# Attention with the scores made twice: once by query for their maxima, once by key for the exponentials

## The chip, the core and the metric

The kernel runs on one core of one Trainium2 chip. The metric is device time in microseconds (us) of one execution of the whole program; lower is better. PE is the matrix engine (PEld its weight loads), DVE the vector engine, ACT the scalar engine with the activation functions, POOL the general-purpose engine, SP the engine whose queue issues all DMA transfers of this kernel.

## What is computed

Two layers run over `x` of shape (4, 512, 512), each with a cross mixer and a feed-forward part, each part added to the residual through a tanh gate. Layer 0 is a recurrent "wkv" scan and a feed-forward part with ternary-sign weights and activations quantised in groups of 64. Layer 1 is cross-attention with 16 heads of 32 channels and a ternary linear layer. The change touches the attention alone:

```python
q = _qdq(x) @ _qdq(wq).T + bq            # x: layer-normed residual, (4, 512, 512)
kv = cond @ wkv.T + bkv
k, v = jnp.split(kv, 2, axis=-1)          # 16 heads of 32 channels each
scale = 1.0 / np.sqrt(Dh)
attn = jax.nn.softmax(jnp.einsum('bnhd,bmhd->bhnm', q, k) * scale, axis=-1)
o = jnp.einsum('bhnm,bmhd->bnhd', attn, v).reshape(B, N, C)
out = _qdq(o) @ _qdq(wp).T + bp           # _qdq: round to int8 steps and back
```

## The kernel before

The four batches pass through the stages one behind the other. While batch b is in attention, batch b+1 is in its feed-forward part and batch b+2 in its scan; the main program walks along a line of places (`line`, `place`, `run`) and lets each generator make its next step when its place comes. The last batch's attention (`alone`) has no feed-forward part beside it. Within PE the order of these steps is fixed: the helpers `matmul` (L162) and `transpose` (L165) put every PE instruction behind those of the step before (`in_turn`, `next_turn`), so a PE instruction that waits holds up all that follow. The other engines also take their instructions in order, and SP issues DMAs in order.

Attention of a batch is 16 units of work: 8 pairs of heads (p), each for two halves of the 512 queries (h); a unit is 2 heads (i) by 2 tiles of 128 queries (t). Queries and keys are kept in DRAM as two parts each, a rounded one and its remainder, so that a product of the fast type float32r keeps accuracy. `stack` (L892) loads them as stacked row blocks of 32: keys as (0, 1, 0, 1), queries as (0, 0, 1, 1), four DMAs each, so that one product over 128 rows sums all four cross terms.

A unit takes these steps, over three turns of the unit loop (L1041 to L1079):

- `scores` (L916): for each i and t one product of 128 queries by 512 keys into a PSUM bank of the group "hp" (3 banks, shared with the feed-forward part's `ff_hp`); DVE takes each row's negated maximum (`at_nm`, L927); ACT takes exp with that as bias, sums the row on the way and writes the weights with queries on partitions (`at_P`, L929).
- `turned` (L937), one turn later: PE transposes the weights, four 128x128 blocks for each i and t, into a bank of group "m" (3 banks; "acc" when alone), and ACT copies them to SBUF (`at_PT`, L949); when alone, DVE makes half of the copies (L947).
- `values` (L952), two turns later: 16 products with 32 columns of V each, four of them side by side in the array (each is two PE instructions in the profile), then an ACT copy (`at_os`).
- `collect` (L971): one transpose back, a reciprocal of the row sums and a product by it (DVE, into `at_o`).

`fetch_queries` asks for the queries of unit k+2, `fetch_keys` for the keys of the next pair of heads. The feed-forward part loads its weights (`wT`, 1 MB each, L704) through the same SP queue; its products are `ff_hp` and `ff_acc`, its transposes `tp_ps`. `qr_ps`, `sx_ps`, `q_ps`, `p_ps`, `f_ps` belong to the projections before and after attention.

Of the kernel before, what the change touches and what calls it, by code (L numbers as in the profile page):

```python
# [10 lines left out]
F32 = mybir.dt.float32  # L11
F32R = mybir.dt.float32r
# [4 lines left out]
ALU = mybir.AluOpType  # L17
# [4 lines left out]
P = 128  # L22
# [8 lines left out]
def kernel(  # L31
# [42 lines left out]
    QSCALE = 1.0 / math.sqrt(DH)  # L74
    GS = 64
    ROWS = 3
    NG = D // GS

    cp = ctx.enter_context(tc.tile_pool(name="const", bufs=1))
# [81 lines left out]
    def matmul(*args, **kwargs):  # L161
        return in_turn(nc.tensor.matmul(*args, **kwargs))  # L162

    def transpose(*args):
        return in_turn(nc.tensor.transpose(*args))  # L165

    def blocks(a):
        return a.rearrange("p (c q) -> p c q", q=P)
# [651 lines left out]
    def attention_layer(b, xb, pool, tiles=range(NT)):  # L820
# [40 lines left out]
        qR, kR, V, PT, sums, made, lanes, out_s = {}, {}, {}, {}, {}, {}, {}, {}  # L861

        def rows(a):
            return slice(DH * a, DH * (a + 1))
# [24 lines left out]
        def stack(dst, src, order):  # L889

            for a, i in enumerate(order):
                nc.sync.dma_start(  # L892
                    out=dst[rows(a), :, :].bitcast(F32),
                    in_=src[i].rearrange("(j p) t -> p j t", p=DH),
                )

        def pair(p):
            return slice(64 * (p % 2), 64 * (p % 2) + 64)

        def fetch_keys(p):  # L900
            kR[p] = pool.tile([P, 2, T], F32R, name="at_kR", tag="at_kR")
            stack(kR[p], kD[b][p // 2][:, pair(p), :], (0, 1, 0, 1))

        def fetch_queries(k):
            p, h = units[k]
            qR[k] = pool.tile([P, 2, 2 * P], F32R, name="at_qR", tag="at_qR", bufs=3)
            at = lo + 2 * P * h
            stack(qR[k], qD[b][p // 2][:, pair(p), at : at + 2 * P], (0, 0, 1, 1))

        def fetch_values(g):  # L910
            V[g] = pool.tile([P, NT, P], F32, name="at_V", tag="at_V")
# [4 lines left out]
        def scores(k, i, t):  # L916

            p, h = units[k]
            if k not in sums:
                sums[k] = sm.tile([P, 2, 2], F32, name="at_sum", tag="at_sum")  # L920
            at = t * P
            sp = psum_tile("s_ps", "hp")
            matmul(
                sp, lhsT=qR[k][:, i, at : at + P], rhs=kR[p][:, i, :], start=True, stop=True
            )
            nm = sm.tile([P, 1], F32, name="at_nm", tag="at_nm", bufs=8)
            nc.vector.tensor_reduce(nm, sp, AX.X, ALU.max, negate=True)  # L927
            lanes[k, i, t] = pool.tile([P, T], F32, name="at_P", tag="at_P", bufs=6)
            nc.scalar.activation(  # L929
                lanes[k, i, t],  # L930
                sp,
                AF.Exp,
                bias=nm,
                accum_out=sums[k][:, t, i : i + 1],
            )

        def turned(k, i, t):  # L937

            if k not in PT:
                PT[k] = pool.tile([P, 2, NT, 2 * P], F32, name="at_PT", tag="at_PT", bufs=1)  # L940
            w = lanes.pop((k, i, t))
            pt = psum_tile("pt_ps", "acc" if alone else "m")
            for m in range(NT):
                transpose(pt[:, m * P : (m + 1) * P], w[:, m * P : (m + 1) * P], ident)
            dst = PT[k][:, i, :, t * P : (t + 1) * P]
            if alone and i:
                made[k] = nc.vector.tensor_copy(dst, blocks(pt))  # L947
            else:
                made[k] = nc.scalar.copy(dst, blocks(pt))  # L949

        def values(k):


            p, h = units[k]
            acc = bank("o_ps")[:, 0:P]
            for m in range(NT):
                for i in range(2):
                    for t in range(2):
                        mm = matmul(
                            acc[rows(2 * i + t), :],  # L960
                            lhsT=V[p // 2][:, m, rows(2 * (p % 2) + i)],
                            rhs=PT[k][:, i, m, t * P : (t + 1) * P],
                            start=(m == 0),
                            stop=(m == NT - 1),
                        )
                        behind(mm, made[k])
            del PT[k]
            out_s[k] = pool.tile([P, P], F32, name="at_os", tag="at_os", bufs=1)
            nc.scalar.copy(out_s[k], acc)  # L969

        def collect(k):  # L971

            p, h = units[k]
            pt = bank("ot_ps")[:, 0:P]
            transpose(pt, out_s.pop(k), ident)
            rt = sm.tile([P, 2, 2], F32, name="at_rt", tag="at_rt")
            nc.vector.reciprocal(rt, sums.pop(k))
            at = tiles[0] + 2 * h
            nc.vector.tensor_tensor(
                o_all[:, at : at + 2, p * 64 : p * 64 + 64].rearrange(  # L980
                    "p t (i d) -> p t i d", d=DH
                ),
                pt.rearrange("p (i t d) -> p t i d", i=2, d=DH),
                rt.unsqueeze(3).to_broadcast([P, 2, 2, DH]),
                ALU.mult,
            )
# [51 lines left out]

        for k in range(len(units) + 2):  # L1041
            now, before = k < len(units), 0 < k <= len(units)
            for i in range(2):
                if now:
                    scores(k, i, 0)
            yield
            if k > 1:
                values(k - 2)
            next_turn()
            for i in range(2):  # L1050
                if before:
                    turned(k - 1, i, 0)
            if alone and k > len(units):
                next_turn()
                next(ahead)
            yield
            for i in range(2):
                if now:
                    scores(k, i, 1)
            yield  # L1060
            for i in range(2):
                if before:
                    turned(k - 1, i, 1)
            next_turn()
            if k > 1:
                collect(k - 2)
            if now:
                p, h = units[k]
                if h == 0:
                    if p + 1 < NP:  # L1070
                        fetch_keys(p + 1)
                    if p % 2 == 0 and p // 2 + 2 < NC:
                        next_turn()
                        project(p // 2 + 2)
                elif p % 2 and p // 2 + 1 < NC:
                    fetch_values(p // 2 + 1)
                if k + 2 < len(units):
                    fetch_queries(k + 2)
            yield  # L1079

        if alone:
# [313 lines left out]
```

## Time and profile before

| | |
|---|---|
| median of 3 runs | 1110.24 us (1108.35 to 1112.83) |
| the profiled execution | 1115.4 us, span 1113.6 us |
| PE busy | 946.8 us (85%) |
| DVE busy | 851.9 us (76%) |
| ACT busy | 704.8 us (63%) |
| POOL busy | 315.3 us (28%) |
| mean granted PE clock | 0.953 |

The span is one execution as the hardware profiler saw it. The busy shares are averages over stages of different make. The first product of attention starts at 380 us; the attention of the four batches begins at about 380, 588, 810 and 983 us, and from 983 us on there is no other batch beside it. In a row of the trace's timeline, the first number is the start (us from the span's start), the second the time from the first instruction's start to the last one's end; matmuls overlap their neighbours, so the price of a burst on PE is read from its start to the start of what follows. Behind "|" or in brackets stands idle time before an instruction and what ended it.

### The profile page before, as it was taken

What the parts mean: (1) busy time and instruction counts of PE and PEld (TensorE: products, weight loads), DVE (VectorE), ACT (ScalarE), POOL (GpSimd) and SP (SyncE); (2) the same over time, 40 slices, a digit from 0 to 9 for tenths busy, and PEclk for the clock granted to TensorE, in tenths of its full rate; (3) what the DMA queues carried; (4) which work ended last, traced back from release to release, by engine and by line L of the source; (5) the groups of instructions that cost most, each with busy time, mean ns of one, the idle gap of its engine ahead of it and who ended that gap; (6) DMA issues with size and microseconds to landing.
All of it is one profiled execution on the core that took longest, in us unless ns stands there. A gap on an engine that the chain in (4) does not pass through costs nothing.

```text
span 1113.6 us, 17974 instructions
## 1 busy us (share of the span) xinstructions
PE 946.8 (85%) x6380; PEld 683.5 (61%) x6380; DVE 851.9 (76%) x1642; ACT 704.8 (63%) x1454; POOL 315.3 (28%) x311
## 2 busy tenths in 40 slices
PE   4879998978878978889998777899998989878885
PEld 3345565555546756667776466677776767656652
DVE  4986447779776799988759988877687766679977
ACT  6756655453224676667777667577775677877864
POOL 3822104432105143542214536412113321100000
PEclk8879999998888999999999999999998999989997
DMA  8189854554435655644746544466564653253411
GB/s 283 50 275 319 305 199 147 179 170 152 151 104 170 226 188 161 195 152 158 246 153 209 178 152 152 145 213 199 170 197 152 225 193 109 71 158 106 114 49 39
DMA packets 85673, 189.68 MB, mean 170 GB/s; under 512 B 12240, under 2 KB 36816, under 8 KB 74576
## 3 DMA queue, kind: packets, MB, share of 16 engines
q1 hardware_dynamic: 85584, 188.53, 51.5%
q8 instruction: 51, 0.84, 0.3%
q14 instruction: 38, 0.31, 0.1%
HBM read 148.65 MB, written 39.85 MB: 169 GB/s over the span
## 4 chain that ended last, share of the span: by engine, by line
PE 44%; DVE 25%; ACT 12%; issue 8%; POOL 6%; DMA 3%; SPq 1%; POOLq 0%; ACTq 0%; DVEq 0%
PE ff_hp L162 13%; PE ff_acc L162 6%; PE pt_ps L165 5%; PE o_ps L162 4%; PE s_ps L162 3%; PE v_ps L162 3%; DVE wk_q L620 3%; ACT at_P L929 3%; DVE at_nm L927 3%; ACT at_PT L949 2%; PE k_ps L162 2%; PE tp_ps L165 2%; DVE wk_p L614 2%; DVE qg_i L660 1%; PE qr_ps L165 1%
## 5 line engine op out<-in xcount | busy, mean ns | idle before, releaser
L162 PE MATMUL ff_hp<-wT,xp 128*128 128x512 f32 x1024 | 273.7, 411 | 3.7 <-ACT at_P L929 2.1
L162 PEld LDWEIGHTS ff_hp<-wT,xp 128*128 128x128 f32 x1024 | 197.4, 196 | 52.4 <-ACT at_P L929 3.8
L929 ACT ACTIVATE at_P<-s_ps,at_nm 128x512 f32<-128x512 f32 x256 | 174.6, 689 | 74.6 <-DVE at_nm L927 70.9
L927 DVE TENSOR_REDUCE at_nm<-s_ps 128x1 f32<-128x512 f32 x256 | 165.6, 676 | 37.8 <-PE s_ps L162 37.2
L665 POOL TENSOR_TENSOR ff_z<-qg_b,qg_s 128x512 f32<-128x512 bf16 x64 | 71.4, 1116 | 333.0 <-ACT qg_b L664 286.6
L165 PE MATMUL pt_ps<-ident,at_P 128*128 128x128 f32 x1024 | 141.1, 278 | 17.5 <-ACT at_os L969 6.6
L949 ACT COPY at_PT<-pt_ps 128x512 f32<-128x512 f32 x224 | 124.5, 595 | 39.7 <-PE pt_ps L165 38.5
L165 PEld LDWEIGHTS pt_ps<-ident,at_P 128*128 128x128 f32 x1024 | 113.2, 140 | 45.6 <-issue 9.3
L162 PE MATMUL ff_acc<-wT,hr 128*128 128x512 f32 x512 | 136.9, 408 | 4.9 <-ACT hr L676 3.0
L162 PE MATMUL s_ps<-at_kR,at_qR 128*128 128x512 f32 x256 | 98.8, 455 | 22.2 <-ACT at_P L929 14.6
L162 PEld LDWEIGHTS ff_acc<-wT,hr 128*128 128x128 f32 x512 | 92.6, 190 | 25.5 <-ACT hr L676 4.1
L725 ACT ACTIVATE ff_z<-ff_hp,coef 128x512 f32<-128x512 f32 x64 | 43.9, 687 | 65.8 <-PE ff_hp L162 63.2
L162 PE MATMUL o_ps<-at_PT,at_V 128*32 128x128 f32 x2048 | 72.2, 279 | 1.3 <-DVE hr L677 0.7
L664 ACT CAST qg_b<-qg_i 128x512 bf16<-128x512 int8 x80 | 49.3, 617 | 35.3 <-DVE qg_i L660 27.4
L162 PEld LDWEIGHTS s_ps<-at_kR,at_qR 128*128 128x128 f32 x256 | 46.2, 196 | 38.7 <-ACT at_P L929 23.6
L730 DVE SCALAR_TENSOR_TENSOR ff_z<-ff_hp,coef,ff_z 128x512 f32<-128x512 f32 x64 | 47.5, 743 | 28.2 <-PE ff_hp L162 28.2
L162 PE MATMUL v_ps<-wkvT,cT 128*128 128x512 f32 x128 | 63.8, 646 | 5.6 <-DVE wT L301 2.3
L162 PEld LDWEIGHTS o_ps<-at_PT,at_V 128*32 128x32 f32 x2048 | 53.8, 111 | 23.9 <-issue 12.2
L726 DVE SCALAR_TENSOR_TENSOR ff_z<-ff_z,ff_hp 128x512 f32<-128x512 f32 x64 | 43.4, 678 | 29.7 <-ACT ff_z L725 29.1
L165 PE MATMUL tp_ps<-ident,ff_z 128*128 128x128 f32 x256 | 41.3, 286 | 26.3 <-ACT at_PT L949 11.3
L162 PE MATMUL k_ps<-cT,wkvT 128*128 128x512 f32 x128 | 60.1, 620 | 3.1 <-ACT cT L444 1.4
L676 ACT CAST hr<-tp_ps 128x512 fp32r<-128x512 f32 x64 | 37.6, 587 | 35.8 <-PE tp_ps L165 35.5
(180 smaller groups left out, 1683.1 us busy)
## 6 DMA issues: line engine op xcount, KB each, us to landing
wT<-wD SPq DMA_DIRECT2D x72, 1024.0 KB, 5.3
wn<-in_L_ffn_w_dram SPq DMA_DIRECT2D x18, 1024.0 KB, 6.3
at_kR<-kD SPq DMA_DIRECT2D x128, 128.0 KB, 3.2
at_qR<-qD SPq DMA_DIRECT2D x256, 64.0 KB, 2.3
wD<-wT SPq DMA_DIRECT2D x12, 1024.0 KB, 4.5
kD<-k_half SPq DMA_DIRECT2D x16, 512.0 KB, 3.0
qD<-at_half SPq DMA_DIRECT2D x32, 256.0 KB, 2.1
cn<-in_ctx_dram SPq DMA_DIRECT2D x8, 512.0 KB, 6.3
```

The lines of the kernel that those rows point to most:

```text
L162: return in_turn(nc.tensor.matmul(*args, **kwargs))
L165: return in_turn(nc.tensor.transpose(*args))
L620: nc.vector.reciprocal(half, half)
L664: nc.scalar.copy(qb, qi)
L665: nc.gpsimd.tensor_tensor(grouped(src), grouped(qb), s.unsqueeze(2).to_broadcast([P, NG, GS]), ALU.mult)
L676: nc.scalar.copy(part[:, 0, :], pt)
L725: nc.scalar.activation(z, hp, AF.Tanh, scale=coef[:, 0:1])
L726: nc.vector.scalar_tensor_tensor(z, z, 1.0, hp, ALU.add, ALU.mult)
L730: nc.vector.scalar_tensor_tensor(z, hp, coef[:, 1:2], z, ALU.mult, ALU.mult)
L927: nc.vector.tensor_reduce(nm, sp, AX.X, ALU.max, negate=True)
L929: nc.scalar.activation(lanes[k, i, t], sp, AF.Exp, bias=nm, accum_out=sums[k][:, t, i : i + 1],)
L949: made[k] = nc.scalar.copy(dst, blocks(pt))
```

## The change

The scores are made twice. The first product, over three row blocks (96 rows) instead of four, serves DVE's maxima alone. `lowered` then splits the unit's four negated maxima in two parts (two DVE operations on 128x4), turns them by one PE transpose into rows (`nt_ps`), lets ACT copy the 8x128 result (`at_nT`, one buffer), and sends it by two small SP DMAs into rows 96 and 97 of the queries' tile. POOL writes ones into rows 96 and 97 of the keys' tile. `weights` makes the second product with keys as output rows and queries as columns, over 98 rows, so that the maximum is already subtracted: 8 products of 128x256 a unit. ACT takes exp with no bias and no sum and so writes the turned weights itself. `turned` and its transposes and copies are gone. `values` makes 16 further products, with ones in the place of V, for the row sums; `collect` has two transposes and takes the reciprocal from PSUM. Keys and queries are three DMAs a tile instead of four; key tiles have 3 buffers instead of 2, query tiles 5 instead of 3, `at_PT` 3 of half the size instead of 1.

With a feed-forward part beside it, a unit still spans three turns; when alone, it spans four (`weights` two turns behind `scores`, `values` three), so there are 19 turns instead of 18.

```diff
         def fetch_keys(p):
-            kR[p] = pool.tile([P, 2, T], F32R, name="at_kR", tag="at_kR")
-            stack(kR[p], kD[b][p // 2][:, pair(p), :], (0, 1, 0, 1))
+            kR[p] = pool.tile([P, 2, T], F32R, name="at_kR", tag="at_kR", bufs=3)
+            nc.gpsimd.memset(kR[p][K3:K5, :, :].bitcast(F32), 1.0)
+            stack(kR[p], kD[b][p // 2][:, pair(p), :], (0, 1, 0))
...
         def scores(k, i, t):
...
             matmul(
-                sp, lhsT=qR[k][:, i, at : at + P], rhs=kR[p][:, i, :], start=True, stop=True
-            )
-            nm = sm.tile([P, 1], F32, name="at_nm", tag="at_nm", bufs=8)
-            nc.vector.tensor_reduce(nm, sp, AX.X, ALU.max, negate=True)
-            lanes[k, i, t] = pool.tile([P, T], F32, name="at_P", tag="at_P", bufs=6)
-            nc.scalar.activation(
-                lanes[k, i, t],
                 sp,
-                AF.Exp,
-                bias=nm,
-                accum_out=sums[k][:, t, i : i + 1],
-            )
-        def turned(k, i, t):
...
-            for m in range(NT):
-                transpose(pt[:, m * P : (m + 1) * P], w[:, m * P : (m + 1) * P], ident)
...
+                lhsT=qR[k][0:K3, i, at : at + P],
+                rhs=kR[p][0:K3, i, :],
+                start=True,
+                stop=True,
+            )
+            nc.vector.tensor_reduce(
+                tops[k][:, i, t : t + 1], sp, AX.X, ALU.max, negate=True
+            )
+        def lowered(k):
+            nm = tops.pop(k).rearrange("p i t -> p (i t)")
+            two = sm.tile([P, 2, 4], F32, name="at_two", tag="at_two")
+            nc.vector.tensor_copy(two[:, 0, :].bitcast(F32R), nm)
+            nc.vector.tensor_tensor(
+                two[:, 1, :].bitcast(F32R), nm, two[:, 0, :], ALU.subtract
+            )
+            pt = bank("nt_ps")[0:8, 0:P]
+            transpose(pt, two.rearrange("p h a -> p (h a)"), ident)
+            turned = pool.tile([8, P], F32, name="at_nT", tag="at_nT", bufs=1)
+            nc.scalar.copy(turned, pt)
+            for h in range(2):
+                nc.sync.dma_start(
+                    out=qR[k][K3 + h : K3 + h + 1, :, :].rearrange(
+                        "h i (t q) -> h (i t) q", q=P
+                    ).bitcast(F32),
+                    in_=turned[4 * h : 4 * h + 4, :],
+                )
+        def weights(k, i):
+            p, h = units[k]
+            PT[k, i] = pool.tile([P, NT, 2 * P], F32, name="at_PT", tag="at_PT", bufs=3)
+            for half in range(2):
+                sp = psum_tile("st_ps", "acc" if alone else "m")
+                for j in range(2):
+                    m = 2 * half + j
+                    matmul(
+                        sp[:, j * 2 * P : (j + 1) * 2 * P],
+                        lhsT=kR[p][0:K5, i, m * P : (m + 1) * P],
+                        rhs=qR[k][0:K5, i, :],
+                        start=True,
+                        stop=True,
+                    )
+                made[k] = nc.scalar.activation(
+                    PT[k, i][:, 2 * half : 2 * half + 2, :].rearrange("p m t -> p (m t)"),
+                    sp,
+                    AF.Exp,
+                )
...
         def values(k):
...
+            for part in range(2):
+                for m in range(NT):
+                    for i in range(2):
+                        for t in range(2):
+                            mm = matmul(
+                                acc[rows(2 * i + t), part * P : (part + 1) * P],
+                                lhsT=ones[:, 0:DH]
+                                if part
+                                else V[p // 2][:, m, rows(2 * (p % 2) + i)],
+                                rhs=PT[k, i][:, m, t * P : (t + 1) * P],
...
         def collect(k):
...
-            nc.vector.reciprocal(rt, sums.pop(k))
+            nc.vector.reciprocal(rt, pt[:, 1, :, :, 0])
...
-        for k in range(len(units) + 2):
...
+        for k in range(count + 3) if alone else ():
             for i in range(2):
-                if now:
+                if within(k):
                     scores(k, i, 0)
             next_turn()
+            if within(k - 1):
+                lowered(k - 1)
+            yield
+            if within(k - 3):
+                values(k - 3)
+            next_turn()
+            if within(k - 2):
+                weights(k - 2, 0)
...
+        for k in range(0 if alone else count + 2):
             for i in range(2):
+                if within(k):
+                    scores(k, i, 0)
             next_turn()
+            if within(k - 1):
+                lowered(k - 1)
+            yield
+            if within(k - 2):
+                values(k - 2)
+            yield
+            for i in range(2):
+                if within(k):
+                    scores(k, i, 1)
+            next_turn()
+            if within(k - 1):
+                weights(k - 1, 0)
+            yield
+            if within(k - 1):
+                weights(k - 1, 1)
...
-            (start, end, 72),
+            (start, end, 72) if b < NB - 1 else (start, end, 76),
```

More of the change, by code (lines that the diff above doesn't have):

```diff
@@ L76 @@
     ROWS = 3
+    QBUFS = 5
     NG = D // GS
@@ L859, in attention_layer @@
             yield from in_steps([prepared(t, r), prepared(t + 1, r)], 1)
-        qR, kR, V, PT, sums, made, lanes, out_s = {}, {}, {}, {}, {}, {}, {}, {}
+        qR, kR, V, PT, tops, made, out_s = {}, {}, {}, {}, {}, {}, {}
+        K3, K5 = 3 * DH, 3 * DH + 2
         def rows(a):
@@ L900, in fetch_keys @@
         def fetch_keys(p):
-            kR[p] = pool.tile([P, 2, T], F32R, name="at_kR", tag="at_kR")
-            stack(kR[p], kD[b][p // 2][:, pair(p), :], (0, 1, 0, 1))
+            kR[p] = pool.tile([P, 2, T], F32R, name="at_kR", tag="at_kR", bufs=3)
+            nc.gpsimd.memset(kR[p][K3:K5, :, :].bitcast(F32), 1.0)
+            stack(kR[p], kD[b][p // 2][:, pair(p), :], (0, 1, 0))
         def fetch_queries(k):
             p, h = units[k]
-            qR[k] = pool.tile([P, 2, 2 * P], F32R, name="at_qR", tag="at_qR", bufs=3)
+            qR[k] = pool.tile([P, 2, 2 * P], F32R, name="at_qR", tag="at_qR", bufs=QBUFS)
             at = lo + 2 * P * h
-            stack(qR[k], qD[b][p // 2][:, pair(p), at : at + 2 * P], (0, 0, 1, 1))
+            stack(qR[k], qD[b][p // 2][:, pair(p), at : at + 2 * P], (0, 0, 1))
         def fetch_values(g):
@@ L918, in scores @@
             p, h = units[k]
-            if k not in sums:
-                sums[k] = sm.tile([P, 2, 2], F32, name="at_sum", tag="at_sum")
+            if k not in tops:
+                tops[k] = sm.tile([P, 2, 2], F32, name="at_nm", tag="at_nm")
             at = t * P
@@ L923, in scores @@
             matmul(
-                sp, lhsT=qR[k][:, i, at : at + P], rhs=kR[p][:, i, :], start=True, stop=True
-            )
-            nm = sm.tile([P, 1], F32, name="at_nm", tag="at_nm", bufs=8)
-            nc.vector.tensor_reduce(nm, sp, AX.X, ALU.max, negate=True)
-            lanes[k, i, t] = pool.tile([P, T], F32, name="at_P", tag="at_P", bufs=6)
-            nc.scalar.activation(
-                lanes[k, i, t],
-                sp,
-                AF.Exp,
-                bias=nm,
-                accum_out=sums[k][:, t, i : i + 1],
-            )
@@ L937, in turned @@
-        def turned(k, i, t):
[L939 to L942, printed above, removed]
-            for m in range(NT):
-                transpose(pt[:, m * P : (m + 1) * P], w[:, m * P : (m + 1) * P], ident)
[L945 to L949, printed above, removed]
+                sp,
@@ new lines, in weights @@
+        def weights(k, i):
[14 more added lines that the diff above has]
+                    PT[k, i][:, 2 * half : 2 * half + 2, :].rearrange("p m t -> p (m t)"),
+                    sp,
+                    AF.Exp,
+                )
@@ L951, in values @@
         def values(k):
             p, h = units[k]
[L955 to L964, printed above, removed]
-                        )
-                        behind(mm, made[k])
@@ L967, in values @@
-            del PT[k]
-            out_s[k] = pool.tile([P, P], F32, name="at_os", tag="at_os", bufs=1)
+            acc = bank("o_ps")[:, 0 : 2 * P]
+            for part in range(2):
[8 more added lines that the diff above has]
+                                rhs=PT[k, i][:, m, t * P : (t + 1) * P],
+                                start=(m == 0),
+                                stop=(m == NT - 1),
+                            )
+                            behind(mm, made[k])
@@ L969, in values @@
+            del PT[k, 0], PT[k, 1]
+            out_s[k] = pool.tile([P, 2 * P], F32, name="at_os", tag="at_os", bufs=1)
             nc.scalar.copy(out_s[k], acc)
@@ L973, in collect @@
             p, h = units[k]
-            pt = bank("ot_ps")[:, 0:P]
-            transpose(pt, out_s.pop(k), ident)
+            pt = bank("ot_ps")[:, 0 : 2 * P]
+            o = out_s.pop(k)
+            for part in range(2):
+                cut = slice(part * P, (part + 1) * P)
+                transpose(pt[:, cut], o[:, cut], ident)
+            pt = pt.rearrange("p (s i t d) -> p s t i d", s=2, i=2, d=DH)
             rt = sm.tile([P, 2, 2], F32, name="at_rt", tag="at_rt")
-            nc.vector.reciprocal(rt, sums.pop(k))
+            nc.vector.reciprocal(rt, pt[:, 1, :, :, 0])
             at = tiles[0] + 2 * h
@@ L982, in collect @@
                 ),
-                pt.rearrange("p (i t d) -> p t i d", i=2, d=DH),
+                pt[:, 0],
                 rt.unsqueeze(3).to_broadcast([P, 2, 2, DH]),
@@ L1037, in attention_layer, with fetches, within @@
         ending = in_steps([ahead, behind_it], 1)
-        for k in range(len(units) + 2):
-            now, before = k < len(units), 0 < k <= len(units)
+        def fetches(k):
+            p, h = units[k]
+            if h == 0:
+                if p + 1 < NP:
+                    fetch_keys(p + 1)
+                if p % 2 == 0 and p // 2 + 2 < NC:
+                    next_turn()
+                    project(p // 2 + 2)
+            elif p % 2 and p // 2 + 1 < NC:
+                fetch_values(p // 2 + 1)
+            if k + 2 < len(units):
+                fetch_queries(k + 2)
+        count = len(units)
+        def within(k):
+            return 0 <= k < count
+        for k in range(count + 3) if alone else ():
             for i in range(2):
-                if now:
+                if within(k):
                     scores(k, i, 0)
+            next_turn()
+            if within(k - 1):
+                lowered(k - 1)
             yield
-            if k > 1:
-                values(k - 2)
+            if within(k - 3):
+                values(k - 3)
             next_turn()
[L1050 to L1053, printed above, removed]
+            if within(k - 2):
+                weights(k - 2, 0)
+            if k == count + 2:
                 next_turn()
@@ L1057, in attention_layer @@
             for i in range(2):
-                if now:
+                if within(k):
                     scores(k, i, 1)
             yield
+            if within(k - 2):
+                weights(k - 2, 1)
+            next_turn()
+            if within(k - 3):
+                collect(k - 3)
+            if within(k):
+                fetches(k)
+            yield
+        for k in range(0 if alone else count + 2):
             for i in range(2):
-                if before:
-                    turned(k - 1, i, 1)
+                if within(k):
+                    scores(k, i, 0)
             next_turn()
-            if k > 1:
-                collect(k - 2)
[L1067 to L1078, printed above, removed]
+            if within(k - 1):
+                lowered(k - 1)
+            yield
+            if within(k - 2):
+                values(k - 2)
+            yield
+            for i in range(2):
+                if within(k):
+                    scores(k, i, 1)
+            next_turn()
+            if within(k - 1):
[3 more added lines that the diff above has]
+                weights(k - 1, 1)
+            next_turn()
+            if within(k - 2):
+                collect(k - 2)
+            if within(k):
+                fetches(k)
             yield
```

## The prediction

> **What bounds the kernel now.** First the page's busy shares, then the windows by stage (length, then busy us of each engine, granted clock, DMA share, GB/s).
>
> ```profile
> PE 946.8 (85%) x6380; PEld 683.5 (61%) x6380; DVE 851.9 (76%) x1642; ACT 704.8 (63%) x1454; POOL 315.3 (28%) x311
> ```
>
> ```profile
> 395.00:500.00 105.00, 85.13 (x619) 66.59 (x617) 95.45 (x157) 69.89 (x150) 50.25 (x48) 0.97 0.57 182
> 500.00:590.00 90.00, 84.80 (x680) 67.18 (x681) 64.57 (x143) 66.35 (x148) 17.14 (x16) 1.00 0.56 185
> 795.00:960.00 165.00, 156.06 (x1208) 122.19 (x1207) 118.43 (x262) 111.10 (x250) 34.82 (x34) 0.98 0.54 174
> 983.00:1083.00 100.00, 86.61 (x921) 62.03 (x922) 85.27 (x184) 75.64 (x193) 1.02 (x1) 0.97 0.37 104
> ```
>
> Three regimes. With the scan beside it (395 to 500, and likewise 595 to 700; 16 units) DVE is 91% busy and sets the pace. In most of the rest of the shared stretches (30 units; two lie in between) PE is 94% busy. The last batch (16 units) has no full engine: it is a loop of waits. The PE timeline gives prices, each from a burst's start to the next start:
>
> ```profile
> 781.76 0.63 PE L162 MATMUL s_ps<-at_kR,at_qR 128*128 128x512 f32 x2
> 782.23 1.99 PE L162 MATMUL ff_hp<-wT,xp 128*128 128x512 f32 x8
> 784.05 1.04 PE L165 MATMUL pt_ps<-ident,at_P 128*128 128x128 f32 x8
> 784.92 0.27 PE L165 MATMUL ot_ps<-ident,at_os 128*128 128x128 f32 x1
> 788.94 1.08 PE L162 MATMUL o_ps<-at_PT,at_V 128*32 128x128 f32 x32
> 789.95 1.09 PE L165 MATMUL pt_ps<-ident,at_P 128*128 128x128 f32 x8
> ```
>
> A score product costs 0.47/2 = 0.235 us, a transpose 0.87/8 = 0.109, a unit's value products 1.01. The last batch, all engines:
>
> ```profile
> 1067.42 0.48 PE L162 MATMUL s_ps<-at_kR,at_qR 128*128 128x512 f32 x1
> 1068.48 0.50 PE L162 MATMUL s_ps<-at_kR,at_qR 128*128 128x512 f32 x1 [0.58 <-ACT at_P L929]
> 1069.22 1.26 DVE L927 TENSOR_REDUCE at_nm<-s_ps 128x1 f32<-128x512 f32 x2
> 1065.72 0.69 DVE L947 COPY at_PT<-pt_ps 128x512 f32<-128x512 f32 x1 [1.26 <-PE pt_ps L165]
> ```
>
> The second score of a pair starts 1.06 us behind the first, not 0.235: its bank is held until ACT's exp is done. The chain of waits in order of time shows the period there:
>
> ```profile
> 1057.91 1.01 PE o_ps L162 x32
> 1063.64 1.01 PE o_ps L162 x32
> 1074.63 1.01 PE o_ps L162 x32
> ```
>
> Three units from 1057.91 to 1074.63: 5.57 us each where nothing else is mixed in, 5.9 from 1045.19 on.
>
> **PE, shared stretches.** Out go 16 transposes, 16 x 0.109 = 1.74 us a unit. In come 8 products of 256 columns: half a score product each, 0.118, so 0.94 (no trace row has this width; the upper bound is a full product's price, 1.88; below half it can't go, since the columns are as many). The products with ones are a second burst like the first: +1.01. One transpose for the maxima and one more at the end: +0.22. Sum +0.43 us a unit, at most +1.37. Over the 30 units that PE bounds that is +13 us. The score products keep their price: 96 rows or 128, the columns are 512. In the DVE-bound units PE has 20% idle and hides it.
>
> The Trainium skill, Perfetto Trace Analysis, § Identifying the Most-Contended Engine, warns that matmul busy time says little about how near PE is to its limit, since matmuls are pipelined; by that the 94% is flattery and the 13 could be near 0. The rows agree in part: 500 to 590 needs, at the prices above, about 79 of its 90 us, but the other 11 are waits of an in-order queue, which added work does not fill by itself, so I keep 13. What may go of these waits: PE waited for `at_P` to free score banks 14.6 us in all, 7.0 of it in the last batch; the new bank is free after DVE's maximum. I take -4 for the shared part. The 11.3 us for which `tp_ps` waited on `at_PT` stay, because an exp stands where the copy stood.
>
> **ACT.** Out: four exps with bias and sum, 0.66 us from start to start, and four copies at 0.55 (two in the last batch, where DVE makes the others). In: four plain exps (no such row; between a copy's 0.55 and the old 0.66), a copy of 8x128 (at most the 0.27 of `at_os`) and an `at_os` of twice the width (between 0.27 and the 0.60 of a 512-wide copy). ACT falls from 5.1 to about 3.2 us a unit. It was 67 to 76% busy and not the limit of any stage: worth nothing beyond the waits just counted.
>
> **DVE.** In the shared stretches two operations on 128x4 are added (0.16 each by the 128x4 rows), the four maxima stay: 0.32 x 16 DVE-bound units = +5. POOL's 32 writes of ones come a pair of heads ahead into a third buffer; POOL is 28% busy; nothing.
>
> **The new round trip.** Between maxima and `st_ps` stand: DVE's two operations, a PE transpose, an ACT copy, an SP issue, a DMA. I read its cover from the order of the built program's instructions, priced as above. Behind `nt_ps` come ACT's copy (0.27), the issue (0.43) and the landing:
>
> ```profile
> at_qR<-qD SPq DMA_DIRECT2D x256, 64.0 KB, 2.3
> ```
>
> (1.7 at the least, 6.8 at the most.) With the transpose's 0.27, 3.3 us at the median. On PE 6.2 to 6.7 us of other work lie between `nt_ps` and the first `st_ps` in most shared units; 4.2 to 4.6 in nine; 2.6 to 3.1 in four (the end of the third batch, no feed-forward left). No DMA ahead of it in SP's queue waits for a PE instruction behind `nt_ps`, so weights loads that wait for a buffer don't block it. Four units at about 1 us, and the slowest tenth of landings: +5 (0 to +20). In front of `nt_ps` PE waits for DVE: mostly 1.6 to 2.4 us of queue against 3.9 to 6 us of PE work, but in three DVE-bound units 9 against 4 to 5. DVE's lateness is already its bound there: +2 (0 to +12).
>
> **The last batch.** The order of PE in a turn is s_ps x2, nt_ps, o_ps, st_ps x4, s_ps x2, st_ps x4, ot_ps x2; DVE's is two maxima, reciprocal, maximum, product, maximum, the two small ones. So `nt_ps` waits for this turn's first pair of maxima and all behind it waits for `nt_ps`. Round the loop: `nt_ps` 0.11, o_ps 2.0, st_ps 0.47, a score and its hand-over 0.44 (781.76 to DVE's start at 782.20), two maxima 1.29, reciprocal 0.17, maximum 0.65, product 0.28, maximum 0.65, two small 0.32, hand-over 0.1: 6.5 us. If the next scores come earlier than the reciprocal, 6.2; if ACT's exps hold the two "acc" banks, 6.7. DVE loses its two copies (1.38 us) and gains nothing by it, since it is now a link of a loop. Against 5.6 to 5.9: +0.75 x 15 = +11 (+4 to +16). The extra turn: from the last unit's first scores (1073.1) to its value products (1082.9) it took 9.8 us; now a turn of 6.5, then two of o_ps 2.0 and four exps (2.4), up to the last products: 15.3. So +6.
>
> The Trainium skill, TensorE: Matmul & The Clock Gate, Part 4: PE-mode transpose, says that transposes don't count as busy for the clock gate, so fewer of them should raise the clock; the granted clock was already 0.97 to 1.00 in these stretches, which leaves 3% of the last 100 us at most.
>
> **Sum.** 13 - 4 + 5 + 5 + 2 + 11 + 6 = +38. The profiled execution took 1115.4 us (span 1113.6), 5.2 above the median; the sum on the median 1110.24 gives 1148. My own case runs from +10 (no round-trip waits, last batch +4) to +70.
>
> **Rivals.**
> 1. *Faster: the banks decide.* PE's lost time sits in front of banks that ACT holds, and ACT is freed of 2 us a unit. If `nt_ps` waits less than 1 us a turn, the last batch's period comes near PE's own load (0.94 + 0.11 + 2.0 + 0.94 + 0.22 = 4.2, and 0.5 for other work): -0.9 x 15 = -13, +6 for the extra turn. If half of the 12% that PE loses over the 345 us of the PE-bound stretches goes too, -20, against +13 on PE and +5 on DVE: -9 in all, 1101. Against it: DVE's order in that loop. Chance 0.20.
> 2. *Slower: the round trip shows everywhere.* A transfer issued behind a 1 MB weights load (5.3 us to land) is late even against 6.2 us. At 2 us for each of 48 units, +96 on part of my sum: 1205. It decides if landings pass 5 us. Chance 0.10.
> 3. *Slower: narrow products at the full price.* If 256 columns cost 0.235, since each brings its own weight load (mean 0.196 for `s_ps`), +0.94 x 30 = +28, +5 in the loop: 1181. For it: the loads; against it: in the transposes' rows a product each 0.109 us with a load each. Chance 0.10.
>
> That the change doesn't do what it says is excluded by the order of instructions: 8 st_ps and twice the o_ps products stand in each unit.
>
> **How the numbers follow.** My case has 0.60. About 0.5% (5.5 us) is what a measurement can tell from no change. Faster: 0.17 of rival 1. Same: 0.03 of rival 1 and 0.04 of my lower end, 0.07. Slower: 0.56 + 0.20 = 0.76. The range leaves out half of rival 2 and about half of rival 1: 1100 to 1185.
>
> **What would show it.** Right: PE idle before `nt_ps` (releaser DVE `at_two`) of 1.5 us or more a turn behind 983 us; a period of 6.2 to 6.7; `st_ps` 0.12 apart; units between 500 and 590 us longer by some 0.4 us. Wrong: `st_ps` waiting on the DMA into `at_qR` in many shared units (rival 2), `st_ps` 0.2 apart (rival 3), or the last batch's period at 5 (rival 1). A wait in a place not named here would make the sum wrong.

## The result, and the profile after

The changed kernel takes 1210.9 us (median of 4 runs, 1208.8 to 1211.7) against 1110.6 us before: 1.09 times as long, 95% interval 1.0874 to 1.0927. The profiled execution has a span of 1208.5 us. The forecast was slower, but by 38 us and not by 100, and the time lies outside the range.

Where the 94.9 us between the two profiled spans came in is seen from the starts of the first score products (us from the span's start; units 0, 16, 32 and 48 open the four batches, unit 63 is the last):

| | unit 0 | 16 | 32 | 48 | 63 | end |
|---|---|---|---|---|---|---|
| before | 380.0 | 588.1 | 810.0 | 983.1 | 1073.1 | 1113.6 |
| after | 381.5 | 617.5 | 857.4 | 1048.7 | 1162.6 | 1208.5 |
| longer by | +1.5 | +27.9 | +18.0 | +18.2 | +23.9 | +5.4 |

(Each difference is that of the stretch that ends there.) So 64 us fall on the shared stretches, 24 on the 15 turns of the last batch, 5 on its end. The page's busy shares of the changed kernel, and its windows for the stages of the prediction (length, then busy us of PE, PEld, DVE, ACT, POOL, clock, DMA share, GB/s):

```profile
PE 997.4 (83%) x8044; PEld 725.2 (60%) x8044; DVE 852.2 (71%) x1738; ACT 576.5 (48%) x1038; POOL 344.0 (28%) x343
```

```profile
395.00:510.00 115.00, 84.07 (x691) 65.67 (x690) 90.17 (x151) 47.35 (x84) 51.53 (x49) 0.84 0.42 143
521.00:617.00 96.00, 87.77 (x874) 69.27 (x874) 63.38 (x151) 48.31 (x94) 21.14 (x21) 0.96 0.45 156
875.00:1045.00 170.00, 150.68 (x1550) 115.75 (x1549) 107.77 (x263) 74.04 (x146) 42.35 (x41) 0.95 0.36 119
1049.00:1163.00 114.00, 87.06 (x1110) 63.94 (x1108) 68.24 (x175) 47.91 (x97) 6.13 (x6) 0.90 0.25 76
```

PE is busy 51 us more over the kernel; ACT is busy 128 us less, and the kernel is slower all the same. No engine is full any more where DVE had been: in the first window DVE has fallen from 91% to 78%, PE from 81% to 73%, and the granted clock from 0.97 to 0.84. Both engines idle more. The waits of the changed kernel (who waited for whom, us in total, times, longest) say for whom; the first row is priced in run 11:

```profile
POOL at_kR L904 <- PE st_ps L163: 174.9, 20, 23.0
PE nt_ps L166 <- DVE at_two L942: 64.1, 24, 7.4
PEld nt_ps L166 <- DVE at_two L942: 20.3, 9, 4.2
```

Added up over the trace, PE sat idle 57 us in front of `nt_ps` in the shared units and 29 us in the last batch. `st_ps` is nowhere late for a DMA. One of the long waits, from the timeline around 444 us (rows of DVE and PE):

```profile
438.63 0.68 DVE L933 TENSOR_REDUCE at_nm<-s_ps 128x1 f32<-128x512 f32 x1
439.46 0.71 PE L163 MATMUL s_ps<-at_kR,at_qR 96*128 96x512 f32 x2
442.15 0.68 DVE L661 TENSOR_TENSOR qg_i<-ff_z,qg_r 128x512 int8<-128x512 f32 x1
442.74 1.28 DVE L933 TENSOR_REDUCE at_nm<-s_ps 128x1 f32<-128x512 f32 x2
443.94 0.73 DVE L941 CAST at_two<-at_nm 128x4 fp32r<-128x4 f32 x1
444.59 1.21 DVE L580 TENSOR_TENSOR_SCAN wk_o<-wc,wk_k 128x512 f32<-128x512 f32 x1
445.73 0.13 DVE L942 TENSOR_TENSOR at_two<-at_nm,at_two 128x4 fp32r<-128x4 f32 x1
446.00 0.37 PE L166 MATMUL nt_ps<-ident,at_two 128*8 128x128 f32 x1 [5.83 <-DVE at_two L942]
446.03 3.76 PE L163 MATMUL ff_hp<-wT,xp 128*128 128x512 f32 x8
450.58 0.75 DVE L634 SCALAR_TENSOR_TENSOR xb<-wy_ps,gates,xb 128x512 f32<-128x512 f32 x1 [3.90 <-PE wy_ps L166]
```

`at_two` belongs to unit 3, whose last maximum is the row at 438.63. But the maxima at 442.74, the first two of unit 4, stand ahead of it on DVE, and so do a quantiser's steps and a scan that has slipped between its two halves. The products of these maxima, at 439.46, are the last thing that PE did: `nt_ps` stands right behind them. PE, with eight feed-forward products ready to run behind `nt_ps`, stands still for 5.83 us. Then DVE, whose next inputs come from PE, stands still for 3.90. And when PE starts again, its eight products take 3.76 us where they took 1.99 before. The granted clock behind the wait, and that of the same eight products in the kernel before (windows with the columns as above):

```profile
446.10:449.50 3.40, 3.40 (x9) 2.62 (x9) 0.54 (x2) 0.25 (x1) 0.00 (x0) 0.50 0.03 6
```

```profile
782.20:784.10 1.90, 1.90 (x10) 1.50 (x9) 1.29 (x2) 1.90 (x5) 0.00 (x0) 1.00 0.00 0
```

Counted over the trace, `nt_ps` follows directly on the next unit's first two score products in all 60 units that have a next one. In 14 of the 48 shared units DVE has the maxima of these products ahead of `at_two`; these 14 hold 54.7 of the 57 us, the other 34 together 2.

The loop of the last batch, one turn where nothing is mixed in:

```profile
1149.48 0.71 PE L163 MATMUL s_ps<-at_kR,at_qR 96*128 96x512 f32 x2
1150.00 0.69 DVE L933 TENSOR_REDUCE at_nm<-s_ps 128x1 f32<-128x512 f32 x1
1150.61 0.28 DVE L1012 TENSOR_TENSOR at_o<-ot_ps,at_rt 128x128 f32<-128x128 f32 x1
1150.81 0.68 DVE L933 TENSOR_REDUCE at_nm<-s_ps 128x1 f32<-128x512 f32 x1
1151.60 0.17 DVE L942 TENSOR_TENSOR at_two<-at_nm,at_two 128x4 fp32r<-128x4 f32 x1
1151.82 0.27 PE L166 MATMUL nt_ps<-ident,at_two 128*8 128x128 f32 x1 [1.62 <-DVE at_two L942]
1156.06 0.71 PE L163 MATMUL s_ps<-at_kR,at_qR 96*128 96x512 f32 x2
```

From 1149.48 to 1156.06 the turn takes 6.58 us, with the chain that the prediction wrote out.

### The profile page after: what moved, and what is told of

It is laid out like the page before. It is cut to its first block, busy times and chain, and to the rows that moved or that the text cites. A ratio compares the mean times of both kernels' runs of the same rounds, so it can differ in the third digit from the quotient of the medians.

```text
span 1208.5 us, 21192 instructions
## 1 busy us (share of the span) xinstructions
PE 997.4 (83%) x8044; PEld 725.2 (60%) x8044; DVE 852.2 (71%) x1738; ACT 576.5 (48%) x1038; POOL 344.0 (28%) x343
## 4 chain that ended last, share of the span: by engine, by line
PE 52%; DVE 25%; ACT 9%; issue 6%; POOL 5%; DMA 2%; SPq 0%; ACTq 0%; POOLq 0%; DVEq 0%
PE ff_hp L163 16%; PE o_ps L163 9%; PE ff_acc L163 7%; DVE at_nm L933 4%; PE v_ps L163 3%; PE st_ps L163 3%; PE s_ps L163 3%; ACT at_PT L972 2%; PE k_ps L163 2%; PE tp_ps L166 2%; DVE wk_q L621 2%; DVE qg_i L661 2%; PE qr_ps L166 1%; ACT wk_e L593 1%; DVE ff_z L731 1%
## 5 line engine op out<-in xcount | busy, mean ns | idle before, releaser
L163 PE MATMUL ff_hp<-wT,xp 128*128 128x512 f32 x1024 | 293.6, 434 | 0.9 <-DVE xp L678 0.7
L163 PEld LDWEIGHTS ff_hp<-wT,xp 128*128 128x128 f32 x1024 | 204.4, 208 | 47.9 <-issue 4.1
L972 ACT ACTIVATE at_PT<-st_ps 128x512 f32<-128x512 f32 x256 | 138.0, 595 | 108.8 <-PE st_ps L163 108.3
L163 PE MATMUL st_ps<-at_qR,at_kR 98*128 98x256 f32 x512 | 94.3, 302 | 11.6 <-ACT at_PT L972 8.2
L163 PE MATMUL s_ps<-at_kR,at_qR 96*128 96x512 f32 x256 | 93.9, 444 | 10.1 <-DVE at_nm L933 8.6
L163 PEld LDWEIGHTS st_ps<-at_qR,at_kR 98*128 98x128 f32 x512 | 79.9, 196 | 32.4 <-ACT at_PT L972 15.1
L904 POOL MEMSET at_kR<- 2x1024 f32 x32 | 30.2, 947 | 222.7 <-PE st_ps L163 174.9
L166 PE MATMUL nt_ps<-ident,at_two 128*8 128x128 f32 x64 | 19.2, 300 | 85.7 <-DVE at_two L942 64.1
L163 PE MATMUL o_ps<-at_PT,ones 128*32 128x128 f32 x2048 | 71.4, 282 | 0.0
L166 PEld LDWEIGHTS nt_ps<-ident,at_two 128*8 128x8 f32 x64 | 5.4, 85 | 100.4 <-issue 61.9
```

Source lines behind the costliest of these rows:

```text
L904: nc.gpsimd.memset(kR[p][K3:K5, :, :].bitcast(F32), 1.0)
L972: made[k] = nc.scalar.activation(PT[k, i][:, 2 * half : 2 * half + 2, :].rearrange("p m t -> p (m t)"), sp, AF.Exp,)
```

## The experiments

Theory A: PE, which takes its instructions in order, stands still at `nt_ps` until DVE has come to `at_two`. Theory B: the added products slow PE. Theory C: the DMA of the hand-off lands late. Theory D: POOL's writes of ones hold up POOL's other work. The kernels ran in four groups, each beside runs of the kernel before on the same chip (medians 1113 to 1115 us); ratios are to these.

**1. No hand-off.** `lowered` is not called; 96 rows and a fixed factor in the second scores.

```diff
-                lowered(k - 1)
+                tops.pop(k - 1)
...
-                        lhsT=kR[p][0:K5, i, m * P : (m + 1) * P],
-                        rhs=qR[k][0:K5, i, :],
+                        lhsT=kR[p][0:K3, i, m * P : (m + 1) * P],
+                        rhs=qR[k][0:K3, i, :],
...
                     AF.Exp,
+                    scale=1e-3,
```

> The changed kernel without the hand-off: the two small DVE operations, the transpose nt_ps, the ACT copy and the two DMAs are left out; the second scores use 96 rows and exp takes 0.001 of them, so the maximum is not subtracted. All other products stay. Theory A (PE stands still at nt_ps until DVE has come to at_two; the profile of the changed kernel puts 64 us on PE and 20 us on its weight loads there): 1125 to 1145 us. Theory B (the added products themselves make PE slower, nearly all of the 100 us): 1190 us or more. Theory C (the DMA into the query rows lands late, st_ps waits): also fast, but then st_ps of the changed kernel should wait for DMA, of which its waits show little.

Measured: 1102.8 us, 0.9895 of before (0.988 to 0.991). All that the change adds to PE, DVE and POOL beside the hand-off, with the longer pipeline, is faster than before by 1%. The hand-off costs 108 us. Theory B is out as the main cause; A had expected 1125 to 1145, so the hand-off costs more than the 84 us of waits in front of `nt_ps`. Of the 107 us between the two profiled spans (1208.5 and 1101.4) 33 are PE's busy time (997.4 and 964.2 us), and `nt_ps` itself makes 64 x 0.11 = 7 of these.

**2. The kernel before with the hand-off alone.** DVE's two operations, `nt_ps` and the copy at the changed kernel's place; nobody reads the result.

```diff
+            next_turn()
+            if before:
+                lowered(k - 1)
             yield
```

> The kernel before with the hand-off alone added at the same place: two small DVE operations, nt_ps on PE, the ACT copy; no DMA, the result is not used; all else as before. Theory A: slower by 40 to 75 us, about 1150 to 1185. Theory B: 64 transposes of 0.11 and 0.32 us of DVE a unit, at most +20, about 1130.

Measured: 1194.4 us, 1.0713 of before (1.0695 to 1.0731), +80 us, a little above the upper end of A.

**3. The same, with the transpose of an older tile.** The transpose reads the small tile of the unit before; the number of instructions is the same.

```diff
+            twos[k] = two
+            two = twos.pop(k - 1, two)
             pt = bank("nt_ps")[0:8, 0:P]
             transpose(pt, two.rearrange("p h a -> p (h a)"), ident)
```

> The kernel before with the hand-off added as in the earlier run, with one difference: the transpose reads the small tile of the unit before, made a whole turn earlier, so the same instructions are issued but PE has nothing to wait for. Theory A: the 80 us of that run are the wait, and this one takes 1115 to 1130 us (64 x 0.11 us on PE, 64 x 0.32 us on DVE). If the instructions themselves or the PSUM bank cost the time: 1170 or more.

Measured: 1123.1 us, 1.0071 of before (1.0049 to 1.0094). So 71 of the 80 us are the wait for a fresh result, and 8 are left with the instructions alone (0.0071 x 1113). The waits in front of `nt_ps`, first of run 2, then of run 3:

```profile
PE nt_ps L165 <- DVE at_two L944: 54.9, 19, 9.4
PEld nt_ps L165 <- DVE at_two L944: 19.4, 10, 2.4
```

```profile
PE nt_ps L165 <- DVE at_two L944: 9.4, 1, 9.4
```

The one wait left is that of unit 16, the first of its batch, which has no older tile to read.

**4. Without the DMAs.** The changed kernel with `nt_ps` where it was, its copy made, nothing sent; 96 rows and the fixed factor in the second scores, as in run 1.

```diff
-            for h in range(2):
-                nc.sync.dma_start(
...
-                    in_=turned[4 * h : 4 * h + 4, :],
-                )
```

> The changed kernel without the two DMAs of the hand-off alone; DVE's two operations, nt_ps and the ACT copy stay at their places; the second scores use 96 rows and exp takes 0.001 of them, so the maximum is not subtracted. Theory A (the wait is between DVE and PE): within 12 us of the changed kernel's 1211. Theory C (landing or SP's queue): 1150 or less.

Measured: 1214.1 us, the changed kernel's time. Theory C is out for the changed kernel. The waits stay:

```profile
PE nt_ps L166 <- DVE at_two L942: 67.1, 24, 7.4
PEld nt_ps L166 <- DVE at_two L942: 22.5, 10, 4.2
```

**5. The small DVE operations earlier.** `lowered` is cut in two; `split_tops` (the two DVE operations) follows the unit's own last maxima, ahead of the next unit's first ones. On PE nothing moves.

```diff
             for i in range(2):
                 if within(k):
                     scores(k, i, 1)
+            if within(k):
+                split_tops(k)
```

> The changed kernel with the two small DVE operations moved ahead, right behind the last maxima of their own unit; nt_ps stays where it is on PE. Theory A in its narrow form (nt_ps waits because the next scores' maxima stand in front of at_two on DVE): the last batch loses about 1.3 us a turn of its wait, 20 us, and the whole falls to 1175 to 1195. If instead DVE is late anyway at that point: within 10 us of the changed kernel's 1211. Theory B: 1211.

Measured: 1140.7 us, 1.023 of before (1.0213 to 1.0247): two operations of 0.16 us, moved on their engine, bring back 70 us. The narrow form of A was right in its mechanism and much too small in its size: in the trace none of the shared units has the next unit's maxima ahead of `at_two` any more. It expected 20 us, in the last batch alone; that batch gave 19 (its 15 turns take 95.3 us, not 113.9), and the shared stretches 49 (from unit 0 to unit 48 they take 999.0 - 380.7 = 618.3 us, not 1048.7 - 381.5 = 667.2). What is left of the wait:

```profile
PE nt_ps L166 <- DVE at_two L942: 19.2, 22, 1.7
PEld nt_ps L166 <- DVE at_two L942: 8.4, 8, 1.5
```

The longest is 1.7 us, not 7.4.

**6. `nt_ps` behind the value products, two turns for the DMA everywhere**, with the early split of run 5.

```diff
-        for k in range(count + 3) if alone else ():
+        for k in range(count + 3):
...
             if within(k - 3):
                 values(k - 3)
             next_turn()
+            if within(k - 1):
+                lowered(k - 1)
+            next_turn()
             if within(k - 2):
                 weights(k - 2, 0)
```

> As the one before, and nt_ps moved behind the value products on PE; the second scores come two turns behind the first in all batches, not in the last alone, so that the DMA has a turn's time. Theory A: the waits at nt_ps nearly vanish, 1125 to 1150 us. Theory B: 1195 or more. If it falls below 1110, the change itself was worth making and only the place of the hand-off was not.

Measured: 1143.8 us, 1.0261 of before (1.0246 to 1.0277). `nt_ps` hardly waits, and the last batch's 15 turns take 85.5 us instead of 90.0 before: the loop is broken. But the shared stretches are 14 us longer than in run 5 (from unit 0 to unit 48, 632.2 against 618.3).

**7. `nt_ps` one burst later beside the feed-forward part**, at the head of the step with `values`; the early split of run 5, the last batch as in run 6.

```diff
             for i in range(2):
                 if within(k):
                     scores(k, i, 0)
-            next_turn()
+            yield
             if within(k - 1):
                 lowered(k - 1)
-            yield
+            next_turn()
             if within(k - 2):
                 values(k - 2)
```

> The changed kernel with the two small DVE operations right behind their own maxima; beside a feed-forward part nt_ps stands one product burst later on PE, at the head of the step with the value products (before them); in the last batch nt_ps stands behind the value products. Theory A (what counts is how late DVE comes to at_two against PE's place of nt_ps): the waits left in the kernel with the early split (19 us on PE, a few on the weight loads) fall by half or more in the shared stretches, the last batch takes the 85 us from its first to its last unit that it took with both moved, not 95: 1112 to 1128 us. A floor is the 1103 us without any hand-off. If the DMA's landing now shows (st_ps later than nt_ps by less than 4 us of PE work), 1140 or more.

Measured: 1164.7 us, 1.0448 of before (1.0419 to 1.0478): the last of the cases expected. Its waits:

```profile
PE st_ps L163 <- DMA at_qR<-at_nT: 20.3, 15, 3.2
PE ff_hp L163 <- DVE ff_z L731: 10.8, 6, 4.1
```

**8. The same without the DMAs**, to see which of these two it lost to.

> The same cut in the kernel whose nt_ps stands one burst later (1165 us), which lost 24 us against the early split though its waits at nt_ps were gone. If the DMA is what it lost to (st_ps waited 20 us for landings and 8 us for SP): 1125 to 1140. If the wait has moved to other places between DVE and PE (ff_hp and s_ps waiting for DVE to free their banks): 1150 or more.

Measured: 1116.8 us, 1.0025 of before (0.9999 to 1.0052), better than either expectation. At this place the hand-off without its DMA costs 14 us (run 1 has none and takes 1102.8), and its DMA 48: `nt_ps` had been moved out of the reach of one wait and into that of the other.

**9. That place with two turns for the DMA.** `values` and `collect` move back by a turn with the second scores.

```diff
-            if within(k - 1):
-                weights(k - 1, 0)
+            if within(k - 2):
+                weights(k - 2, 0)
...
```

> The kernel with nt_ps one burst later, whose DMA cost it 48 us, with the second scores two turns behind the first in the shared stretches too: nt_ps keeps its late place, the DMA has a whole turn more. If landing time was all that it lost to: near the 1117 us of the same order without the DMAs, 1112 to 1128. If the longer pipeline brings waits of its own (more value products and exps behind it at each batch's end, PSUM banks held otherwise), as in the first kernel with two turns, 1135 or more. Under 1105 would beat both kernels.

Measured: 1145.4 us, 1.0268 of before (1.0225 to 1.0311). `st_ps` no longer waits for the DMA, but only 19 of the 48 us come back. `st_ps` stands 15.3 us in front of PSUM banks that ACT's exps hold (5.1 in run 8), but it did so for 12.7 in run 7 already. The two kernels with two turns everywhere, runs 6 and 9, take about as long in the shared stretches, 632 and 634 us, wherever `nt_ps` stands; that the longer pipeline causes this is argued, not shown.

**10. The best places together:** the shared stretches of run 5, the last batch of run 6.

> The shared stretches as in the kernel with the early split (nt_ps at the changed kernel's place), the last batch as in the kernel with nt_ps behind the value products. If the stages add up: the early split's 999 us to the last batch's first scores, 85 us to its last unit, 43 us for the rest, and 1.5 around: about 1130. If the stages depend on each other's order, more than 1140.

Measured: 1130.6 us, 1.0152 of before (1.0115 to 1.0189). The stages add up as reckoned. It is the fastest kernel with this change, and still slower than the one before; no run beat it with the whole computation in it.

**11 and 12. Two prices.** Without POOL's writes of ones, and without the products with ones, both in the kernel of run 1.

```diff
-            nc.gpsimd.memset(kR[p][K3:K5, :, :].bitcast(F32), 1.0)
```

> The changed kernel without the hand-off, as before, and without POOL's writes of ones into the key tiles (the rows are not read there). Theory D (POOL waits 170 us in front of these writes for st_ps to free a key tile, and holds up what stands behind: the scan and the quantiser): faster than 1103 by 8 us or more. Otherwise, the waits lie in POOL's idle time: within 4 us of 1103.

Measured: 1097.9 us (1091.8 to 1103.0) against 1102.8 (1102.1 to 1104.1), ratios to before 0.9823 to 0.989 and 0.988 to 0.991. The medians lie 5 us apart, between the two cases expected, and the intervals overlap, so it isn't settled whether the writes cost anything; of the 168 us that POOL waits in front of them in run 1 hardly any reaches the kernel's time.

```diff
-            for part in range(2):
+            for part in range(1):
                 for m in range(NT):
...
```

> The changed kernel without the hand-off and without the products with ones and their transpose (the row sums are then not made; the reciprocal reads value columns). It prices PE work in this kernel. If a us of PE work costs a us in the stretches that PE bounds and in the last batch: 46 units x 1.1 = 51, so 1050 to 1060 us. If PE's in-order waits hide half: 1075 to 1085. If PE is not the limit: 1095 or more.

Measured: 1071.4 us, 31 less than with them, a little below the case in which in-order waits hide half. The products and their transpose are 64 x 1.1 = 70 us of PE work, so a us of PE work costs 0.45 us here, as a mean over all stages and with the ACT copy behind them halved too.

## Why the prediction failed

**The step that failed** is the wait "in front of `nt_ps`", put at "+2 (0 to +12)" for the shared stretches. It is the change's main cost: PE's idle time there is 57 us in the shared units and 29 in the last batch, and the hand-off costs 8 us without its wait (run 3) and 80 with it (run 2). In all the forecast had +21 for the shared stretches (13 - 4 + 5 + 5 + 2), and 64 came.

Two errors made the wait small. First, the "3.9 to 6 us of PE work" was taken to cover the queue on DVE. It does so where no maxima of the next unit come in between (34 shared units, 2 us of idling). In the other 14 the next unit's first maxima stand ahead of it, and their products are the ones right in front of `nt_ps` on PE: nothing is left to cover the wait. The prediction saw this loop in the last batch and not here. Secondly, the three units that it did see as late (9 us of queue against 4 to 5 on PE) were dismissed with "DVE's lateness is already its bound there". The longest waits, in units 17, 1, 3 and 4, were 7.4, 6.0, 5.8 and 5.3 us, all in the stretches that DVE bounds. A bound engine stays the bound only while it is fed: with PE stopped in front of `nt_ps`, DVE ran dry behind it (the 3.90 us above), and the two took turns. And PE came back at half its clock.

**The last batch.** The loop was right in its links, its period (6.5 forecast, 6.58 measured) and its rank as the new bound. Its price was mis-sized, +11 against +24: ten of the 15 turns take 63 us instead of 58, but the five longest, all with projections mixed in (8.4 to 12.5 us each), 51 instead of 32. The prediction charged all 15 alike; what makes these five so long is not shown. The extra turn's +6 was 5.4.

**PE's work.** The prices held: from the timeline of the changed kernel,

```profile
425.70 0.64 PE L163 MATMUL st_ps<-at_qR,at_kR 98*128 98x256 f32 x4
426.18 0.39 PE L166 MATMUL ot_ps<-ident,at_os 128*128 128x128 f32 x2
431.23 1.08 PE L163 MATMUL o_ps<-at_PT,at_V 128*32 128x128 f32 x32
432.13 1.06 PE L163 MATMUL o_ps<-at_PT,ones 128*32 128x128 f32 x32
433.12 2.10 PE L163 MATMUL ff_acc<-wT,hr 128*128 128x512 f32 x8
```

a narrow product takes 0.48/4 = 0.12 us (rival 3 is out), the two value bursts 1.89 together. But 13 - 4 + 6 = +15 was charged for all this with the extra turn, and run 1 is 12 us faster than before. Run 12 gives one reason, 0.45 us for a us of PE work; the shared stretches without a hand-off take 599.5 us against 603.0 before. The other is that the waits for ACT's banks did go: without a hand-off the last batch's 15 turns take 77 us instead of 90, and PE idles 3.7 us in them instead of 15.5, of which 10.8 stood in front of score banks and of the banks of the transposes. That was rival 1's mechanism, and its -13 for this batch. It is real and was buried under the hand-off.

**Rival 2** named 1205 us, near the result, by luck: its cause isn't the changed kernel's, whose DMAs cost nothing where they stand (run 4). Runs 7 and 8 show that they do at another place. **POOL's writes** were put at nothing; run 11 leaves some 5 us open. **ACT's relief** shows, as forecast, only in the waits for its banks; that these would shorten the last batch was left to rival 1.

Behind 5.83 us of idling the granted clock is 0.50 and eight products take 3.76 us, not 1.99. The Trainium skill, TensorE: Matmul & The Clock Gate, Part 1, says that the array falls to half its clock after an idle window of about 3.4 us; this row agrees. The prediction used that page only to see whether fewer transposes would raise the clock, and not to ask what a new wait would do to it: the mean clock fell from 0.953 to 0.922.

## What to carry to other kernels

A small result that has to pass from one in-order engine to another and back is priced by the queue in front of its makers, not by its own duration: two operations of 0.16 us and a transpose of 0.11 us in each of 64 units cost 108 us. So look in the built order at what stands ahead of the makers, and whether any of it needs a product that the waiting engine issues just before it waits; then there is no cover at all. Add the new operations where they are first possible, and put the waiting instruction on the other engine where something else has been done in the meantime, with the DMA's time still ahead of it; each move must be tried against both. And an engine that is the bound gives no cover for a new wait of the engine that feeds it.

## What was not expected of the hardware

A wait can be dearer than its length. Runs 2 and 3 issue the same instructions; their profiled spans are 1193.4 and 1117.3 us, with mean granted clocks of 0.921 and 0.964. Of the 76 us between them 35 are not idling but PE's busy time (975.1 and 939.9 us). At one place, eight products of 512 columns behind a 5.83 us wait took 3.76 us at a granted clock of 0.50, instead of 1.99 at 1.00.
